# Running the first MLP on the masked tokens alone in a two-MLP block, and its conditioning as rows

## The chip, the cores and the metric

The kernel runs on one core of a Trainium2 chip. The metric is the device time of one execution in microseconds (us); the median of several runs counts. In one profiled execution every instruction was recorded. Its engines are PE (TensorE, the matmuls), DVE (VectorE), ACT (ScalarE), POOL (GpSimd) and SP (SyncE, which only issues transfers); ACT, POOL and SP each have a queue that issues transfers.

## The reference

32 sequences of 128 tokens with 512 features, all float32. A condition vector of each sequence gives six rows of 512: shift, scale and gate for each of two MLPs. The first MLP stands twice (weights `ssm`, `bwd`) and counts only for tokens whose mask is true; the second counts for all.

```python
m = mask[:, :, None]
shift, scale, gate_msa = jnp.split(silu(t) @ ada_w + ada_b, 3, axis=1)
norm = _layernorm(x) * (1.0 + scale[:, None]) + shift[:, None]
norm = jnp.where(m, norm, 0.0)
fwd = _ssm_fallback(norm, ssm_w1, ssm_b1, ssm_w2, ssm_b2)    # gelu(u @ w1 + b1) @ w2 + b2, 512 -> 512 -> 512
bwd = flip(_ssm_fallback(flip(norm), bwd_w1, bwd_b1, bwd_w2, bwd_b2))
x = x + gate_msa[:, None] * jnp.where(m, fwd + bwd, 0.0)
shift_mlp, scale_mlp, gate_mlp = jnp.split(silu(t) @ ffada_w + ffada_b, 3, axis=1)
ff_norm = _layernorm(x) * (1.0 + scale_mlp[:, None]) + shift_mlp[:, None]
h = gelu_tanh(ff_norm @ ff_w1 + ff_b1)                       # 512 -> 1024
return x + gate_mlp[:, None] * (h @ ff_w2 + ff_b2)
```

The mask comes from the setup: a sequence has between 0 and 32 true tokens, its last ones, and over all 32 sequences 499 of the 4096 are true. The mask is an input, so the kernel learns this only while it runs.

## The kernel before

Both MLPs of the first half work token by token, so the kernel joins them into one with a hidden layer of 1024. It works on eight groups of four sequences (512 tokens), and every group goes through both halves in full; the mask only multiplies the result of the first half, in the last step of `mixed` (L256).

`modulation` (L150) computes the conditioning: shift and scale as columns [feature, sequence] (`pm`, L157), the gate as rows (`pg`, L176), which go to DRAM and come back spread over all partitions by `gate_tiles` (L233). `normalise` (L184) does the LayerNorm of four token tiles on DVE, with the square root on ACT. `hidden` (L203) transposes the normalised tiles on PE into `ptr` (L209), lets ACT evict them with scale and shift (L213), and computes the hidden layer `ph` (L225), eight tiles of 128 features by 512 tokens, each a sum of four matmuls; ACT applies the Gelu (L229). `project` (L240) computes `po`, one token tile, as a sum of eight matmuls (L244); DVE adds the bias and multiplies by the gate (L246, L247). In the trace a program's float32 matmul is two PE instructions. Names end in `_a` or `_m` for the first half and `_b` or `_f` for the second.

The program order of the loop is: the first half's projection of group g, its normalising, the hidden layer of the first half of group g + 1, and then the second half of group g. A scheduler of the framework (Tile) turns this into a fixed order for each engine's queue; it also places the waits. SP's queue issues the loads of `ada_w` and of x, ACT's queue the weights, biases and the mask, POOL's queue the gates and the output.

Of the kernel before, what the change touches and what calls it, by code (L numbers as in the profile page):

```python
# [9 lines left out]
F32 = mybir.dt.float32  # L10
U8 = mybir.dt.uint8
AF = mybir.ActivationFunctionType
ALU = mybir.AluOpType

EPS = 1e-6


@with_exitstack
def kernel(
# [35 lines left out]
    B, S, D = x.shape  # L55
    P = 128
# [22 lines left out]

    ident = const.tile([P, P], F32, name="ident")  # L80
    make_identity(nc, ident)
    eps = const.tile([P, 1], F32, name="eps")
    nc.gpsimd.memset(eps, EPS)

# [1 line left out]
    NB = 3 * KC  # L86
    n_bias = 2 * NB + 2 * KC + HC
    t_sb = tp.tile([B, D], F32, tag="t", name="t_sb")
    nc.sync.dma_start(t_sb, cond)
    bias_rows = const.tile([n_bias, P], F32, name="bias_rows")  # L90
    at = 0
    col = {}
    for key, vec in (
        ("ada", ada_b), ("ffada", ffada_b), ("ssm1", ssm_b1), ("bwd1", bwd_b1), ("ff1", ff_b1)
    ):
# [4 lines left out]
    mask_u8 = const.tile([B, S], U8, name="mask_u8")  # L100
    nc.scalar.dma_start(mask_u8, mask)

    def load_ada(w, j, which):
        chunk = adap.tile([P, KC, D], F32, tag="ada", name=f"ada_{which}_{j}")
        nc.sync.dma_start(chunk, w[:, ts(j, D)].rearrange("(k p) f -> p k f", p=P))
        return chunk

    def load_x(g):
        tiles = []
        for i in range(G):  # L110
            t = xp.tile([P, D], F32, tag="x", name=f"x_{g}_{i}")
            nc.sync.dma_start(t, x[g * G + i])
            tiles.append(t)
        return tiles
# [4 lines left out]
    fw2 = const.tile([P, HC, D], F32, name="fw2")  # L119

# [18 lines left out]
    for key in ("ada", "ffada"):  # L139
        c = biasT[:, col[key] + KC : col[key] + 2 * KC]  # L140
        nc.vector.tensor_scalar(c, c, 1.0, None, ALU.add)

# [199 lines left out]
```

## Time and profile before

| | |
|---|---|
| median of 3 runs | 1005.19 us (1004.99 to 1005.72) |
| span of the profiled execution, first to last instruction | 1003.0 us |
| what lies around the span, taken against the median | 2.2 us |
| PE busy | 953.0 us (95%) |
| DVE, ACT, POOL busy | 220.2, 217.2, 30.4 us (22, 22, 3%) |
| PE matmul instructions | 2454 |
| moved by DMA | 49.77 MB |

The busy share tells which engine is full, not what it waits for; the chain that ended last goes back from the last instruction to whatever released each step. "issue" in it is time in which an engine waited for nothing that the profile shows. PEclk is the clock that was granted to TensorE, as a share of 2.4 GHz: 1.0 is the upper of its two levels and 0.5, 1.2 GHz, the lower.

### The profile page before, as it was taken

The numbers are of one execution on the slowest core, as the hardware profiler recorded it, in microseconds if no ns is written. First come the engines' busy times: TensorE is split into PE (matmuls) and PEld (weight loads), VectorE is DVE, ScalarE is ACT, GpSimd is POOL, SyncE is SP. The second block draws the span as 40 slices with busy tenths as digits, with TensorE's granted clock in tenths as the row PEclk, the third lists the DMA queues.
The fourth block names the chain that finished last, engine by engine and source line by source line (L and its number), as shares of the span: only waits on it lengthen the run. The fifth ranks groups of instructions, "written<-read, shape, count | busy, mean of one in ns | idle before, by whom it ended". The sixth has DMA issues, their size and how long they took to land.

```text
span 1003.0 us, 6139 instructions
## 1 busy us (share of the span) xinstructions
PE 953.0 (95%) x2454; PEld 441.0 (44%) x2454; DVE 220.2 (22%) x411; ACT 217.2 (22%) x427; POOL 30.4 (3%) x62
## 2 busy tenths in 40 slices
PE   5699999999999999999999999999999999999796
PEld 5344444444444444444444444444444444444342
DVE  2202500243002510135002430035101430024202
ACT  0220442004410234004410044102340044200310
POOL 1000000000000000000000000000000000000000
PEclk9799999999999999999999999999999999999899
DMA  9921200021002200022000210021000110001000
GB/s 329 356 80 55 74 0 0 32 77 60 0 1 84 70 15 1 21 74 73 1 0 32 84 54 0 11 73 73 1 1 21 63 42 1 0 32 53 0 6 37
DMA packets 16893, 49.77 MB, mean 50 GB/s; under 512 B 1688, under 2 KB 1728, under 8 KB 14816
## 3 DMA queue, kind: packets, MB, share of 16 engines
q0 software_dynamic: 5232, 26.22, 7.4%
q1 hardware_dynamic: 7824, 14.75, 4.4%
q10 hardware_dynamic: 3808, 8.41, 2.3%
q8 instruction: 19, 0.31, 0.1%
q14 instruction: 10, 0.08, 0.0%
HBM read 40.85 MB, written 8.52 MB: 49 GB/s over the span
## 4 chain that ended last, share of the span: by engine, by line
PE 82%; issue 11%; DMA 3%; ACT 2%; POOL 0%; DVE 0%; ACTq 0%; POOLq 0%
PE ph_a L225 22%; PE ph_b L225 19%; PE po_m L244 19%; PE po_f L244 17%; PE ptr_a L209 1%; DMA ada_ffada<-in_L_cond_ffada_w_dram 1%; DMA ada_ada<-in_L_cond_ada_w_dram 1%; ACT xT_b L213 1%; ACT xT_a L213 1%; PE ptr_b L209 1%; PE pm_ada L157 1%; DMA mask_u<-in_mask_BxS_bk_dram 1%; PE pg_ada L176 1%; ACT h_a L229 0%; PE pg_ffada L176 0%
## 5 line engine op out<-in xcount | busy, mean ns | idle before, releaser
L225 PE MATMUL ph_a<-xT_a,w 128*128 128x512 f32 x512 | 226.7, 600 | 0.0
L225 PE MATMUL ph_b<-xT_b,fw 128*128 128x512 f32 x512 | 225.1, 596 | 0.0
L244 PE MATMUL po_m<-w,h_a 128*128 128x512 f32 x512 | 221.1, 592 | 0.0
L244 PE MATMUL po_f<-fw,h_b 128*128 128x512 f32 x512 | 221.0, 592 | 0.0
L244 PEld LDWEIGHTS po_m<-w,h_a 128*128 128x128 f32 x512 | 97.2, 190 | 122.8 <-issue 122.8
L244 PEld LDWEIGHTS po_f<-fw,h_b 128*128 128x128 f32 x512 | 97.3, 190 | 122.5 <-issue 122.5
L225 PEld LDWEIGHTS ph_a<-xT_a,w 128*128 128x128 f32 x512 | 96.3, 192 | 118.7 <-issue 111.4
L225 PEld LDWEIGHTS ph_b<-xT_b,fw 128*128 128x128 f32 x512 | 95.9, 191 | 117.6 <-issue 111.5
L246 DVE TENSOR_TENSOR t_f<-po_f,fb 128x512 f32<-128x512 f32 x32 | 22.1, 692 | 564.8 <-PE po_f L244 564.8
L213 ACT ACTIVATE xT_a<-ptr_a,modT_ada 128x128 f32<-128x128 f32 x128 | 46.4, 465 | 377.0 <-PE ptr_a L209 377.0
L229 ACT ACTIVATE h_b<-ph_b,biasT 128x512 f32<-128x512 f32 x64 | 44.0, 687 | 146.3 <-PE ph_b L225 146.2
L229 ACT ACTIVATE h_a<-ph_a,biasT 128x512 f32<-128x512 f32 x64 | 44.0, 687 | 142.5 <-PE ph_a L225 142.1
L246 DVE TENSOR_TENSOR t_m<-po_m,b 128x512 f32<-128x512 f32 x32 | 22.1, 692 | 128.6 <-PE po_m L244 128.6
L213 ACT ACTIVATE xT_b<-ptr_b,modT_ffada 128x128 f32<-128x128 f32 x128 | 46.3, 477 | 5.7 <-PE ptr_b L209 5.7
L264 POOL DMA_DIRECT2D out_dram<-x x32 | 17.3, 540 | 662.6 <-DVE x L263 661.2
L209 PE MATMUL ptr_b<-ident,xn_b 128*128 128x128 f32 x128 | 19.8, 291 | 15.3 <-ACT xT_b L213 10.9
L209 PEld LDWEIGHTS ptr_b<-ident,xn_b 128*128 128x128 f32 x128 | 15.4, 147 | 26.6 <-ACT xT_b L213 13.0
L209 PE MATMUL ptr_a<-ident,xn_a 128*128 128x128 f32 x128 | 18.8, 281 | 8.5 <-ACT xT_a L213 8.5
L189 DVE BATCH_NORM_STATS2 st_a<-x 128x6 f32<-128x512 f32 x32 | 21.4, 670 | 17.3 <-DMA x<-in_x_dram 17.3
L256 DVE SCALAR_TENSOR_TENSOR x<-t_m,maskT,x 128x512 f32<-128x512 f32 x32 | 24.1, 752 | 1.1
L209 PEld LDWEIGHTS ptr_a<-ident,xn_a 128*128 128x128 f32 x128 | 15.4, 145 | 19.4 <-ACT xT_a L213 11.6
L189 DVE BATCH_NORM_STATS2 st_b<-x 128x6 f32<-128x512 f32 x32 | 22.2, 695 | 1.1
(55 smaller groups left out, 225.1 us busy)
## 6 DMA issues: line engine op xcount, KB each, us to landing
x<-in_x_dram SPq DMA_DIRECT2D x32, 256.0 KB, 5.1
gate_m<-gate_rows_ada POOLq DMA_DIRECT2D x8, 1024.0 KB, 5.2
gate_f<-gate_rows_ffada POOLq DMA_DIRECT2D x8, 1024.0 KB, 5.6
out_dram<-x POOLq DMA_DIRECT2D x32, 256.0 KB, 2.3
fw<-in_L_cond_ff_w_dram ACTq DMA_DIRECT2D x2, 2048.0 KB, 12.3
ada_ada<-in_L_cond_ada_w_dram SPq DMA_DIRECT2D x3, 1024.0 KB, 7.5
ada_ffada<-in_L_cond_ffada_w_dram SPq DMA_DIRECT2D x3, 1024.0 KB, 10.7
w<-in_L_cond_ssm_w_dram ACTq DMA_DIRECT2D x2, 1024.0 KB, 11.7
```

Of the source, the lines that this page charges most:

```text
L157: nc.tensor.matmul(pm[:, ts(j * KC + c, B)], chunk[:, k, ts(c, P)], sT[:, k, :], start=(k == 0), stop=(k == KC - 1),)
L176: nc.tensor.matmul(pg[:B, :], sT[:, k, :], chunk[:, k, :], start=(k == 0), stop=(k == KC - 1))
L189: nc.vector.bn_stats(st, src[i])
L209: nc.tensor.transpose(ptr[:, ts(i, P)], xn[i][:, ts(k, P)], ident)
L213: nc.scalar.activation(t[:, ts(i, P)], ptr[:, ts(i, P)], AF.Identity, bias=modT[:, k, b : b + 1], scale=modT[:, KC + k, b : b + 1],)
L225: nc.tensor.matmul(ph, w[:, k, ts(f, P)], xT[k], start=(k == 0), stop=(k == KC - 1))
L229: nc.scalar.activation(t, ph, func, bias=biasT[:, bcol + f : bcol + f + 1])
L244: nc.tensor.matmul(po, h[f][:, ts(i, P)], w[:, f, :], start=(f == 0), stop=(f == HC - 1))
L246: nc.vector.tensor_tensor(t, po, bias, ALU.add)
L256: nc.vector.scalar_tensor_tensor(r, t, maskT[:, b : b + 1], xt[i], ALU.mult, ALU.add)
L264: nc.gpsimd.dma_start(out[g * G + i], x1[i])
```

## The change

The first half is done once, for 512 slots. At the start the kernel counts the masked tokens of each sequence, computes with small matmuls against triangles of ones at which slot each sequence begins (`first`) and ends (`behind`), and builds `pick`, a matrix of zeros and ones [sequence, slot], four times one above the other so that each strip of 32 partitions has it. `tokens_of` finds the token of each slot, and the reverse, the slot of each token (`slot_i`, a number beyond 512 for a token that is not masked), comes from running sums (`rank`). Four indirect transfers on POOL's queue gather the 512 rows of x.

The conditioning is computed as rows [3 x 32, 512], shift, scale and gate in three strips of 32 columns of PE's array (`modulation`), and spread to the slots by a matmul with `pick` (`of_slots`). The rows of the first half's result go to DRAM (`x1_rows`). Then the eight groups do the second half only: for each group x is loaded, and four indirect transfers put the rows of `x1_rows` over the masked tokens and leave the others as they are (`take_first_half`). The square root becomes a power on POOL. The stores move from POOL's queue to SP's, the loads of the MLP weights from ACT's queue to SP's. At the end stands a loop whose number of trips, (masked tokens - 512 + 127) // 128 and at least 0, is computed on the chip; a trip takes 128 further masked tokens through both halves.

```diff
+    xp = ctx.enter_context(tc.tile_pool(name="xp", bufs=2 * G + 2))
+    xnp = ctx.enter_context(tc.tile_pool(name="xnp", bufs=G + 2))
+    xtp = ctx.enter_context(tc.tile_pool(name="xtp", bufs=2))
...
+    mask_u8 = const.tile([B, S], U8, name="mask_u8")
+    nc.scalar.dma_start(mask_u8, mask)
...
+    def load_ada(w, which):
+        rows = []
+        for k in range(KC):
+            t = adap.tile([P, 3 * D], F32, tag="ada", name=f"ada_{which}_{k}")
+            nc.sync.dma_start(t, w[ts(k, P), :])
+            rows.append(t)
+        return rows
...
+    for j, w in enumerate((ssm_w1, bwd_w1)):
+        nc.sync.dma_start(w1[:, :, ts(j, D)], w.rearrange("(k p) f -> p k f", p=P))
+    for j, w in enumerate((ssm_w2, bwd_w2)):
+        nc.sync.dma_start(w2[:, ts(j, KC), :], w.rearrange("(k p) f -> p k f", p=P))
...
+    count = const.tile([B, 1], F32, name="count")
+    nc.vector.tensor_reduce(count, mask_f, axis=AX.X, op=ALU.add)
+    pb = ps_t.tile([P, 512], F32, tag="tr", name="pb")
+    nc.tensor.transpose(pb[:, :B], mask_f, ident[:B, :B])
+    for j in range(2):
+        nc.tensor.matmul(
+            pb[:, B + j : B + j + 1],
+            upper[:, j].rearrange("p c b -> p (c b)"),
+            count,
+            start=True,
+            stop=True,
+        )
+    nc.tensor.matmul(pb[:, B + 2 : B + 3], ones_b, count, start=True, stop=True)
...
+    pick = const.tile([P, NS], F32, name="pick")
+    nc.vector.scalar_tensor_tensor(pick, slot_row, first, inside, ALU.is_ge, ALU.mult)
...
+    def tokens_of(picked, slots, n, name):
+        pl = ps_t.tile([P, 512], F32, tag="tr", name=f"pl_{name}")
+        for c in range(n):
+            nc.tensor.matmul(pl[:, ts(c, S)], picked[:B, ts(c, P)], rank, start=True, stop=True)
+        view = pl[:, : n * S].rearrange("p (c s) -> p c s", s=S)
+        before = stp.tile([P, n, S - 1], F32, tag=f"before{n}", name=f"before_{name}", bufs=1)
+        nc.vector.tensor_tensor(
+            before,
+            view[:, :, : S - 1],
+            slots.unsqueeze(2).to_broadcast([P, n, S - 1]),
+            ALU.is_le,
+        )
+        token = stp.tile([P, n], F32, tag=f"token{n}", name=f"token_{name}", bufs=1)
+        nc.vector.tensor_reduce(token, before, axis=AX.X, op=ALU.add)
+        nc.vector.tensor_tensor(token, token, view[:, :, S - 1], ALU.add)
+        return token
...
+    def modulation(rows, modb, which):
+        nc.vector.tensor_scalar(modb[B : 2 * B], modb[B : 2 * B], 1.0, None, ALU.add)
         pm = ps_o.tile([P, 512], F32, tag="o", name=f"pm_{which}")
...
         for k in range(KC):
...
+            for j in range(3):
+                nc.tensor.matmul(
+                    pm[ts(j, B), :],
+                    sT[:, k, :],
+                    rows[k][:, ts(j, D)],
+                    start=(k == 0),
+                    stop=(k == KC - 1),
+                )
+        mod = const.tile([3 * B, D], F32, name=f"mod_{which}")
+        nc.vector.tensor_tensor(mod, pm[: 3 * B, :], modb, ALU.add)
+        return mod
+    def of_slots(picked, c, mod, j, pool, tag, name):
+        t = pool.tile([P, 512], F32, tag=tag, name=name)
+        nc.tensor.matmul(
+            t, picked[ts(j, B), ts(c, P)], mod[ts(j, B), :], start=True, stop=True
+        )
+        return t
...
-        rstd = stp.tile([P, G], F32, tag="rstd", name=f"rstd_{name}")
-        nc.scalar.activation(rstd, mv[:, :, 1], AF.Sqrt, bias=eps)
-        nc.vector.reciprocal(rstd, rstd)
+        ve = stp.tile([P, n], F32, tag=f"ve{n}", name=f"ve_{name}")
+        nc.vector.tensor_scalar(ve, mv[:, :, 1], EPS, None, ALU.add)
+        rstd = stp.tile([P, n], F32, tag=f"rstd{n}", name=f"rstd_{name}")
+        nc.gpsimd.tensor_tensor(rstd, ve, half[:, :n], ALU.pow)
...
+    def modulate_slots(xn, picked, c, mod, name):
+        scale = of_slots(picked, c, mod, 1, ps_o, "o", f"sc_{name}")
+        shift = of_slots(picked, c, mod, 0, ps_o, "o", f"sh_{name}")
+        nc.vector.tensor_tensor(xn, xn, scale, ALU.mult)
+        nc.vector.tensor_tensor(xn, xn, shift, ALU.add)
+    def transposed_slots(xn, dst, name):
+        ptr = ps_t.tile([P, 512], F32, tag="tr", name=f"ptr_{name}")
         for k in range(KC):
...
+            nc.tensor.transpose(ptr[:, ts(k, P)], xn[:, ts(k, P)], ident)
+        nc.scalar.copy(dst, ptr.rearrange("p (k s) -> p k s", s=P))
...
+    def hidden(xT, n, w, bcol, func, name):
         h = []
         for f in range(HC):
-            ph = ps_h.tile([P, 512], F32, tag="h", name=f"ph_{name}_{g}_{f}")
+            ph = ps_h.tile([P, 512], F32, tag="h", name=f"ph_{name}_{f}")
             for k in range(KC):
                 nc.tensor.matmul(
-                    ph, w[:, k, ts(f, P)], xT[k], start=(k == 0), stop=(k == KC - 1)
+                    ph[:, :n], w[:, k, ts(f, P)], xT[:, k, :], start=(k == 0), stop=(k == KC - 1)
...
+    def gather(dst, token_col):
+        nc.gpsimd.indirect_dma_start(
+            out=dst,
+            out_offset=None,
+            in_=x_rows,
+            in_offset=bass.IndirectOffsetOnAxis(ap=token_col, axis=0),
+        )
...
+    xc = []
+    for c in range(NC):
+        t = xp.tile([P, D], F32, tag="x", name=f"xc_{c}")
+        gather(t, token_i[:, c : c + 1])
+        xc.append(t)
...
+    mod1 = modulation(ada_k, modb1, "a")
+    ffada_k = load_ada(ffada_w, "f")
+    modb2 = load_mod_bias(ffada_b, "f")
+    nc.sync.dma_start(fw1, ff_w1.rearrange("(k p) f -> p k f", p=P))
+    nc.sync.dma_start(fw2, ff_w2.rearrange("(k p) f -> p k f", p=P))
...
+    xn = normalise(xc, "c")
+    xT_all = xtp.tile([P, KC, NS], F32, tag="xT", name="xT_c")
+    for c in range(NC):
+        modulate_slots(xn[c], pick, c, mod1, f"c{c}")
+        transposed_slots(xn[c], xT_all[:, :, ts(c, P)], f"c{c}")
+    h1 = hidden(xT_all, NS, w1, col["ssm1"], AF.Gelu, "c")
+    x1_rows = dram.tile([NS, D], F32, name="x1_rows")
+    for c in range(NC):
+        gate = of_slots(pick, c, mod1, 2, ps_h, "h", f"gate_c{c}")
+        t = project(c, h1, w2, b2, gate, "c")
+        nc.vector.tensor_tensor(t, t, xc[c], ALU.add)
+        nc.sync.dma_start(x1_rows[ts(c, P), :], t)
+    mod2 = modulation(ffada_k, modb2, "f")
...
+    def take_first_half(g, tiles):
+        for i in range(G):
+            b = g * G + i
+            nc.gpsimd.indirect_dma_start(
+                out=tiles[i],
+                out_offset=None,
+                in_=x1_rows,
+                in_offset=bass.IndirectOffsetOnAxis(ap=slot_i[:, b : b + 1], axis=0),
+                bounds_check=NS - 1,
+                oob_is_err=False,
...
+    xt = load_x(0)
+    take_first_half(0, xt)
+    xT = transposed(0, normalise(xt, "0"))
     for g in range(NG):
-        more = g + 1 < NG
-        if more:
+        if g + 1 < NG:
             xt_next = load_x(g + 1)
-            xn_next = normalise(xt_next, f"a{g + 1}")
-        x1 = mixed(g, xt, h1, gate_tiles(g, rows1, "m"))
-        xn2 = normalise(x1, f"b{g}")
-        if more:
+            take_first_half(g + 1, xt_next)
+        gate = gate_tiles(g)
+        h2 = hidden(xT, G * S, fw1, col["ff1"], AF.Gelu_apprx_tanh, f"f{g}")
+        if g + 1 < NG:
+            xT = transposed(g + 1, normalise(xt_next, f"{g + 1}"))
+        for i in range(G):
+            t = project(i, h2, fw2, fb2, gate[:, i, :], f"f{g}")
+            nc.vector.tensor_tensor(xt[i], xt[i], t, ALU.add)
+            nc.sync.dma_start(out[g * G + i], xt[i])
...
+    more = nc.values_load(
+        more_i[0:1, 0:1],
+        min_val=0,
+        max_val=(T - NS) // P,
+        skip_runtime_bounds_check_because="it is (the masked tokens - NS + 127) / 128, at least 0",
+    )
+    with tc.For_i(0, more, 1):
...
+        xl = xp.tile([P, D], F32, tag="x", name="xl")
+        gather(xl, tok_i)
...
```

## Rows read from the trace of the kernel before

**Rows 1.** The page's head and first busy table: busy us (share of span) xinstructions.

```profile
span 1003.0 us, 6139 instructions
...
PE 953.0 (95%) x2454; PEld 441.0 (44%) x2454; DVE 220.2 (22%) x411; ACT 217.2 (22%) x427; POOL 30.4 (3%) x62
```

**Rows 2.** The page's chain that ended last, shares of the span by engine.

```profile
PE 82%; issue 11%; DMA 3%; ACT 2%; POOL 0%; DVE 0%; ACTq 0%; POOLq 0%
```

**Rows 3.** Groups by line and shape: count | busy us, mean ns | idle before, releaser.

```profile
L225 PE MATMUL ph_a<-xT_a,w 128*128 128x512 f32 x512 | 226.7, 600 | 0.0
L225 PE MATMUL ph_b<-xT_b,fw 128*128 128x512 f32 x512 | 225.1, 596 | 0.0
L244 PE MATMUL po_m<-w,h_a 128*128 128x512 f32 x512 | 221.1, 592 | 0.0
L244 PE MATMUL po_f<-fw,h_b 128*128 128x512 f32 x512 | 221.0, 592 | 0.0
...
L264 POOL DMA_DIRECT2D out_dram<-x x32 | 17.3, 540 | 662.6 <-DVE x L263 661.2 <-issue 1.3
```

**Rows 4.** The chain in order of time, two halves of groups: start us, us, what.

```profile
201.28 27.47 PE po_m L244 x64
...
233.66 25.90 PE ph_a L225 x60
...
264.59 25.96 PE ph_b L225 x60
290.55 27.47 PE po_f L244 x64
318.01 27.47 PE po_m L244 x64
```

**Rows 5.** The chain in order of time, from the start to the first projection.

```profile
17.16 10.36 DMA ada_ada<-in_L_cond_ada_w_dram
...
27.57 5.84 PE pg_ada L176 x8
...
45.25 0.91 PE ptr_a L209 x4
...
84.48 27.66 PE po_m L244 x64
```

**Rows 6.** Windows at the start and the last group: length, engines' busy us (x), PEclk, DMA share, GB/s.

```profile
10.00:25.00 15.00, 13.96 (x65) 13.76 (x65) 4.66 (x13) 0.41 (x1) 0.00 (x0) 1.00 1.04 387
...
912.00:945.00 33.00, 27.19 (x69) 12.51 (x68) 11.13 (x20) 8.06 (x19) 0.00 (x0) 0.90 0.00 0
```

**Rows 7.** Timeline between the halves of the last group: start, us, instruction [idle before].

```profile
929.14 0.69 DVE L246 TENSOR_TENSOR t_m<-po_m,b 128x512 f32<-128x512 f32 x1 [3.71 <-PE po_m L244]
...
932.32 0.30 ACT L192 ACTIVATE rstd_b<-mv_b,eps 128x4 f32<-128x4 f32 x1 [56.13 <-DVE mv_b L190]
...
932.87 1.91 DVE L197 TENSOR_SCALAR xn_b<-x,mv_b,rstd_b 128x512 f32<-128x512 f32 x4
...
933.47 2.06 PE L209 MATMUL ptr_b<-ident,xn_b 128*128 128x128 f32 x8 [4.37 <-DVE xn_b L197]
...
941.10 9.38 PE L225 MATMUL ph_b<-xT_b,fw 128*128 128x512 f32 x21
```

**Rows 8.** Timeline of the last tile.

```profile
987.65 7.03 PE L244 MATMUL po_f<-fw,h_b 128*128 128x512 f32 x16
...
996.17 0.69 DVE L263 TENSOR_TENSOR x<-x,t_f 128x512 f32<-128x512 f32 x1
```

**Rows 9.** DMA issues: queue xcount, KB each, median us from issue to landing.

```profile
x<-in_x_dram SPq DMA_DIRECT2D x32, 256.0 KB, 5.1
...
out_dram<-x POOLq DMA_DIRECT2D x32, 256.0 KB, 2.3
...
mask_u<-in_mask_BxS_bk_dram ACTq DMA_DIRECT2D x1, 4.0 KB, 6.6
```

**Rows 10.** Waits of SP's queue: total us, times, longest; the line is the kernel's end.

```profile
SPq L337 <- PEq L337: 2.2, 2, 1.8
```

**Rows 11.** Waits of PE: total us, times, longest.

```profile
PE ptr_a L209 <- ACT xT_a L213: 8.5, 7, 1.2
```

More of the change, by code (lines that the diff above doesn't have):

```diff
@@ L92 @@
     col = {}
[L93 to L95 removed]
+    for key, vec in (("ssm1", ssm_b1), ("bwd1", bwd_b1), ("ff1", ff_b1)):
         n = vec.shape[0] // P
@@ L99 @@
         at += n
[L100 to L114, printed above, removed]
     w1 = const.tile([P, KC, FF], F32, name="w1")
@@ new lines @@
+    nc.tensor.matmul(pb[:, B + 2 : B + 3], ones_b, count, start=True, stop=True)
+    mcol = const.tile([P, B + 3], F32, name="mcol")
+    nc.vector.tensor_copy(mcol, pb[:, : B + 3])
+    maskT = mcol[:, :B]
+    first, behind, total = (mcol[:, B + j : B + j + 1] for j in range(3))
+    inside = tp.tile([P, NS], F32, tag="t", name="inside")
+    nc.vector.tensor_scalar(inside, slot_row, behind, None, ALU.is_lt)
+    pick = const.tile([P, NS], F32, name="pick")
+    nc.vector.scalar_tensor_tensor(pick, slot_row, first, inside, ALU.is_ge, ALU.mult)
@@ new lines @@
+    pg = ps_t.tile([P, 512], F32, tag="tr", name="pg")
+    nc.tensor.matmul(pg[:B, :S], maskT, lower, start=True, stop=True)
+    rank = const.tile([B, S], F32, name="rank")
+    nc.vector.tensor_scalar(rank, pg[:B, :S], first[:B], None, ALU.add)
+    slot_of = const.tile([B, S], F32, name="slot_of")
+    nc.vector.tensor_scalar(slot_of, rank, -1.0 - FAR, None, ALU.add)
+    nc.vector.tensor_tensor(slot_of, slot_of, mask_f, ALU.mult)
+    nc.vector.tensor_scalar(slot_of, slot_of, FAR, None, ALU.add)
@@ new lines @@
+    mod2 = modulation(ffada_k, modb2, "f")
+    modT = const.tile([P, KC, 3 * B], F32, name="modT")
+    ptr = ps_t.tile([P, 512], F32, tag="tr", name="ptr_mod")
+    for k in range(KC):
+        nc.tensor.transpose(
+            ptr[:, ts(k, 3 * B)], mod2[:, ts(k, P)], ident[: 3 * B, : 3 * B]
+        )
+    nc.vector.tensor_copy(modT.rearrange("p k c -> p (k c)"), ptr[:, : KC * 3 * B])
+    gate_rows = dram.tile([B, D], F32, name="gate_rows")
+    nc.gpsimd.dma_start(gate_rows, mod2[2 * B : 3 * B, :])
@@ new lines, with load_x @@
+    early.close()
+    gp = ctx.enter_context(tc.tile_pool(name="gp", bufs=2))
+    def load_x(g):
+        tiles = []
+        for i in range(G):
+            b = g * G + i
+            t = xp.tile([P, D], F32, tag="x", name=f"x_{g}_{i}")
+            nc.sync.dma_start(t, x[b])
+            tiles.append(t)
+        return tiles
+    def take_first_half(g, tiles):
+        for i in range(G):
+            b = g * G + i
+            nc.gpsimd.indirect_dma_start(
[5 more added lines that the diff above has]
+                oob_is_err=False,
+            )
@@ new lines, in transposed @@
+    def transposed(g, xn):
+        xT = xtp.tile([P, KC, G * S], F32, tag="xT", name=f"xT_{g}")
+        for k in range(KC):
+            ptr = ps_t.tile([P, 512], F32, tag="tr", name=f"ptr_{g}_{k}")
+            for i in range(G):
+                nc.tensor.transpose(ptr[:, ts(i, P)], xn[i][:, ts(k, P)], ident)
+            for i in range(G):
+                b = g * G + i
+                nc.scalar.activation(
+                    xT[:, k, ts(i, P)],
+                    ptr[:, ts(i, P)],
+                    AF.Identity,
+                    bias=modT[:, k, b : b + 1],
+                    scale=modT[:, k, B + b : B + b + 1],
+                )
+        return xT
@@ new lines @@
+        if g + 1 < NG:
+            xT = transposed(g + 1, normalise(xt_next, f"{g + 1}"))
+        for i in range(G):
+            t = project(i, h2, fw2, fb2, gate[:, i, :], f"f{g}")
+            nc.vector.tensor_tensor(xt[i], xt[i], t, ALU.add)
+            nc.sync.dma_start(out[g * G + i], xt[i])
+        if g + 1 < NG:
+            xt = xt_next
+    row_l = const.tile([P, P], F32, name="row_l")
+    nc.vector.tensor_scalar(row_l, slot_row[:, :P], float(NS), None, ALU.add)
+    col_l = const.tile([P, 1], F32, name="col_l")
```

244 lines of the change are left out of this document (133 added, 111 removed).

## The prediction

> **What bounds the kernel now.** I read the page's head and busy table first: PE is busy 95% of the span [rows 1]. The chain of waits gives the same engine: 82% of what ended last is PE, and most of the other 11%, "issue", is PE's spacing between its own matmuls [rows 2]. The groups by line then say on what: four groups of 512 matmuls take 221 to 227 us each, the two layers of the first MLP (ph_a, po_m) and the two of the second (ph_b, po_f), and the two MLPs cost the same [rows 3]. One matmul of the program is two PE instructions, so 512 are 8 groups of sequences x 64.
>
> The chain in order of time gives the rate: 64 po instructions take 27.47 us, 0.429 us each. From one po_m to the next, 318.01 - 201.28 = 116.73 us go by [rows 4]. Of these 4 x 64 x 0.429 = 109.9 us are MLP matmuls and 6.8 us transposes and PE's wait for ACT, which evicts them: 3.4 us for each of the two halves. So a half of a group costs 58.4 us, and only PE's work counts in the steady part: DVE, ACT and POOL are busy at most a quarter of the span [rows 1]. The rest is a start of 112.1 us until the first po_m ends [rows 5], a gap where the last group has no other half beside it [rows 7], and a tail [rows 8].
>
> **The change, part by part.** The mask of the reference's inputs holds 499 true tokens of 4096 (counted from its setup code). They fit in 512 slots, so the computed trip count is (499 - 512 + 127) // 128 = 0, and the loop's body does not run.
>
> *Removed.* Eight first halves become one of 512 slots: 7 x 58.4 = 408.6 us of PE's path go. The Sqrt on ACT goes too, with its table loads; they lay beside PE's work and count for nothing.
>
> *Groups.* Each group is now 64 ph and 64 po, 54.9 us, or 55.1 with the slightly longer ph (27.6). For seven of them the 16 transposes of the next group come between. With today's waits they cost 3.4 us; 1.2 of it PE waits for ACT's evictions [rows 11], so packed they cost 2.2. Today PE has nothing else ready at that place; afterwards the po matmuls of the current group are ready while ACT evicts. I take 2.4, near the packed end: 8 x 55.1 + 7 x 2.4 = 457.6 us (456.2 to 464.6). Under one group lie four loads of x (5.1 us), four gathers, four stores and the normalising of the next group (some 6 us of DVE: four statistics of 0.9, xn 1.9, a power); the hidden layer alone covers 27 us. The stores move from POOL's queue to SP's, where loads queue behind stores that wait for DVE. With ten x buffers the last two loads of group g+1 need the stores of group g-1, and those are out by the middle of that group's projection, so a load is half a group early. On POOL, the gate load and the power for 1/sqrt stand behind gathers that wait for the loads; who waits for them are DVE (xn, then PE's transposes) and the gate multiply, both half a group later. Without this cover, a late gather would be late for the transposes directly.
>
> *Front.* Today the first hidden layer effectively starts 27.6 before its po, near 57 us [rows 5]. Afterwards: the mask is the first transfer on ACT's queue and lands at 3 to 7 us (6.6 us behind six others today [rows 9]). The chain of counting, picking and searching is some 25 DVE and PE steps in turn: four DVE passes over 512 columns at 0.69 [rows 8], 21 short ones at 0.3 (932.32 to 932.87 holds two with their handover [rows 7]), 9 us, and 2 more for PE at the lower clock: 11. The tokens stand at 14 to 19 us, and I take 16. Four gathers of 256 KB: no row has one. Below, it is a plain POOL issue, 0.54 us [rows 3], with the 2.3 us to landing of a 256 KB store; above, each takes 5.1 us like a load of x among other transfers, one behind the other [rows 9]. I take 1.2 us of POOL each, nearer the plain issue because only the row addresses differ, and 4 us to land, since transfers run at 387 GB/s [rows 6] with the weights: all landed at 25. Then the last tile's statistics 0.9, power 0.7, four xn 1.9 [rows 7], eight multiplies and adds from PSUM 5.5, transposes and copy 2: the first hidden layer starts at 36 us (30 to 46).
>
> The conditioning is 24 instructions over 512 columns a time. The row pg_ada, 8 such in 5.84 us, 0.73 each [rows 5], is at a mixed clock; at 0.43 to 0.85 they are 10.3 to 20.5 us in turn. They start as rows of ada_w land, 4 to 12 us, and are done before the first xn is there, at some 27: hidden by the gathers, in the bad case +6 on the front. The first MLP's weights move from ACT's queue to SP's, behind ada_w: 3 + 4 MB at 387 GB/s are 18 us, over before 36.
>
> The Trainium skill (TensorEngine Tiling (Array Packing), Key Properties) says that tiles of the array work independently and in parallel; by that rule the three strips of one k overlap and the 24 cost some 3.4 us at the 0.43 rate. pg_ada is one strip alone, so no row here shows it. By either price the sum is 590, as the gathers end later; by the rule the front's upper end would be 40 instead of 46.
>
> *First half.* 27.6 for ph, 27.5 for po, four gate products of two instructions 3.4, and 3.4 for a PE that restarts at the 1.2 GHz level after idling (clock 0.90 over 33 us is 6.6 us at half rate [rows 6]): 61.9, so until 97.9 us.
>
> *Seam.* The groups need the first half's rows, which now go through DRAM. Today's last group shows the same seam without DRAM: the last po_m is evicted from 929.14 and ph_b streams from 941.10, of which four ph (1.7) are work: 10.4 us lost [rows 7]. The change adds a store (0.4 + 2.3 [rows 9]) and four gathers, 4 x 1.2 + 2.5 = 7.3 (4.5 with plain issues; 20 one behind the other). So 20.4 (14 to 34). The second conditioning, 10.3 us of PE, fits into it, and would cost that much ahead of the projection.
>
> *Tail.* From the last po_f's end, 987.65 + 7.03 = 994.68, to 1003.0 are 8.3 us [rows 8]. The loop of no trips adds reading a number on each engine, synchronising them at its entry and exit and a jump over its body. No row has one. Below it is nothing; the nearest row is the end's own meeting of engines, 2.2 us for two [rows 10]; above I put 15. I take 4.
>
> *Sum.* 36 + 61.9 + 20.4 + 457.6 + 8.3 + 4 = 588.2 us of span. The profiled execution's span is 1003.0 against a median of 1005.2; with these 2.2 us around it: **590 us**, 41% less.
>
> **Rivals.**
> A, the groups wait. If gathers cost POOL 5 us each and start late, or loads stand behind stores on SP, the transposes wait in every group, 5 to 12 us: seven times that is 35 to 84, so 625 to 675 us. For it: four gathers, a power and a gate load in one queue, and SP's mixed order. Against it: the half group of cover. 12%.
> B, front and seam go better than I take them: gathers at the plain issue price, conditioning inside the gaps, a front of 28 and a seam of 12. Then 590 - 8 - 8 - 3 (first half at full clock) - 1 (packed transposes) = 570, down to 558 with no loop cost and a warm start. 15%.
> C, one trip runs because the mask timed holds over 512 tokens. Its chain: tokens and gather some 17, and two halves of some 26 each (64 instructions of 128 columns at a quarter of 0.43 or a little more, 16 of 512, and 10 us of small steps in turn), so about 70: 660 us. Against: 499 counted. 3%.
> D, a dear tail. The loop's entry waits until the last stores have landed, and the jump over the body finds no code ready and waits for a transfer. Two transfers in turn at the dearest small one, 6.6 us [rows 9], are 13 instead of 4: 599 us. For it: nothing lies beside the kernel's end. Against it: no wait of that kind is in the rows. 14%. The Trainium skill (Runtime: NRT & Kernel Launch, Instruction fetch mechanics) speaks for it: code is fetched in sequence, and a taken branch to a page not held waits for a DMA fetch. No row here has a branch, so the trace neither bears it out nor speaks against it.
> E, slower than before: the row gathers. There are 36, four in each group; a group hides about 27 us of them. To lose the whole gain of 415 us, eight groups must each wait 52 us: 79 us for four, some 20 us a gather. The nearest row is 0.54 us of POOL [rows 3] and 2.3 to 5.1 to land [rows 9]. 1%.
>
> **How the numbers follow.** The forecast, 575 to 622, has 55%, and D lies inside its range. The ends of its terms (30 or 46; 14 or 34; 456.2 or 464.6; 0 or 15 for the loop) would not all meet. The low end 566 takes in half of B; the high end 628 stops in A's beginning, so about 17% stays outside. A difference of 0.2% (2 us) is about what a measurement of this kernel can tell from none; all cases but E are far beyond it: faster 98.5%, same 0.5%, slower 1%.
>
> **What would show it.** Right: 64 ph and 64 po instructions for the first MLP and 512 of each for the second; a distance of about 57.5 us from one group's po to the next; one long PE gap between the halves with store, gathers and normalising in it; no instruction of the loop's body. A wait of PE's transposes on xn inside the groups, behind a gather, would show A. Wrong it would be through a gather's price, which stands in the front, the seam and A at once, or through an order of PE's queue that puts the second conditioning ahead of matmuls whose inputs are there.

## The result and the profile after

After: 602.81 us (median of 4 runs, 601.39 to 603.9) against 1005.09, a ratio of 0.5998 [0.5988, 0.6007]: 40% faster. The forecast of 590 is 12.8 us too low; 602.8 lies inside its range of 566 to 628. The loop made no trip.

The page's head and busy table of after:

```profile
span 600.9 us, 3810 instructions
...
PE 547.7 (91%) x1395; PEld 246.7 (41%) x1395; DVE 137.5 (23%) x263; ACT 101.2 (17%) x208; POOL 60.4 (10%) x73
```

The bound is still PE, with 405 us less of busy time than in [rows 1]; its idle time grew from 50 to 53 us and is now in three places. Windows of after, with the columns of [rows 6]: gathering the masked rows, modulating them, the first half, the seam, one group, and the end.

```profile
22.00:36.00 14.00, 8.14 (x30) 1.81 (x24) 4.26 (x11) 0.00 (x0) 4.99 (x5) 0.82 1.03 416
36.00:51.48 15.48, 10.75 (x27) 5.00 (x27) 6.72 (x12) 2.38 (x5) 0.00 (x0) 0.50 0.94 372
51.48:113.27 61.79, 61.79 (x136) 25.71 (x136) 6.21 (x9) 6.74 (x9) 0.00 (x0) 0.97 0.08 26
113.27:140.48 27.21, 11.08 (x49) 5.21 (x49) 14.90 (x34) 4.30 (x12) 14.69 (x15) 0.62 0.32 109
195.76:252.45 56.69, 56.69 (x146) 25.89 (x145) 14.56 (x28) 11.09 (x24) 5.73 (x6) 1.00 0.19 60
590.84:600.90 10.06, 0.00 (x0) 0.00 (x0) 2.08 (x3) 0.00 (x0) 0.00 (x0) 0.67 0.08 29
```

In the first half and in a group PE is busy for every microsecond, nearly all of it at the upper clock level (0.97 and 1.00). Ahead of the first half and in the seam it stands still for long, and runs at the lower level (0.50) when it is needed. The stretches against the prediction's terms, in us:

| term | forecast | measured | from which rows |
|---|---|---|---|
| front, until the first hidden layer | 36 | 51.5 | window 3 begins at 51.48 |
| first half | 61.9 | 61.8 | its length |
| seam | 20.4 | 25.5 | 27.21 less 1.72 for four ph inside |
| groups | 457.6 | 452.1 | 590.84 - 140.48 + 1.72 |
| tail and loop | 12.3 | 10.1 | last window |
| sum (span) | 588.2 | 600.9 | |

**The front.** Timeline of after from the mask to the first hidden layer; a bracket gives the engine's idle time before the instruction and what ended it:

```profile
7.77 0.42 DVE L266 TENSOR_SCALAR modb_a<-modb_a 32x512 f32<-32x512 f32 x1 [4.42 <-DMA modb_a<-in_L_cond_ada_b_dram]
...
10.53 0.42 DVE L266 TENSOR_SCALAR modb_f<-modb_f 32x512 f32<-32x512 f32 x1 [2.34 <-DMA modb_f<-in_L_cond_ffada_b_dram]
10.97 0.20 DVE L195 COPY mcol<-pb 128x35 f32<-128x35 f32 x1
...
18.84 0.69 DVE L367 TENSOR_TENSOR b<-b,b2b 128x512 f32<-128x512 f32 x1 [4.93 <-DMA b2b<-in_L_cond_bwd_b_dram]
...
21.77 0.16 DVE L237 CAST token_i<-token_s 128x4 int32<-128x4 f32 x1
...
26.12 0.95 POOL L352 DMA_INDIRECT xc<-in_x_dram,token_i  x1 [0.30 <-issue]
...
33.40 0.69 DVE L296 BATCH_NORM_STATS2 st_c<-xc 128x6 f32<-128x512 f32 x1 [0.88 <-DMA xc<-in_x_dram,token_i]
...
35.75 1.46 DVE L305 TENSOR_SCALAR xn_c<-xc,mv_c,rstd_c 128x512 f32<-128x512 f32 x3 [1.24 <-POOL rstd_c L301]
...
51.48 5.80 PE L331 MATMUL ph_c<-xT_c,w 128*128 128x512 f32 x9 [0.68 <-ACT xT_c L323]
```

Three instructions that have nothing to do with the tokens stand in DVE's queue among the steps of the token chain: the `+ 1` on the two conditioning biases (L266) and the sum of the first MLP's two output biases (L367). Each waits for a transfer, and the token chain waits behind it: `mcol` starts at 10.97, and the tokens (`token_i`) are there at 21.9. POOL is done with the gathers at 27.1, 5.1 us after the tokens (4.8 forecast), but the last rows are there at 33.4. From the normalised rows to the first hidden layer 15.7 us go by, and DVE waits in it for scale and shift out of PE (its wait rows):

```profile
DVE xn_c L316 <- PE sh_c L284: 3.6, 2, 2.7
DVE xn_c L316 <- PE sc_c L284: 3.2, 1, 3.2
```

**The groups.** Chain in order of time, one period (against 116.73 us for two halves in [rows 4]):

```profile
195.76 27.47 PE ph_f L331 x64
223.23 0.87 PE ptr L430 x8
224.10 1.72 PE po_f L345 x4
225.82 0.44 PE ptr L430 x4
...
252.45 27.47 PE ph_f L331 x64
```

The transposes come in lots between projections, as forecast, and cost 1.75 us (56.69 less two times 27.47). No wait of PE for a gather is in this chain; it is DVE's statistics that wait for the gathers, off the chain.

**The seam.** Timeline of after:

```profile
118.87 1.09 POOL L416 DMA_INDIRECT x<-x_rows,slot_i  x1 [0.31 <-issue]
...
127.63 0.17 DVE L299 TENSOR_SCALAR ve<-mv 128x4 f32<-128x4 f32 x1
...
128.13 1.01 POOL L416 DMA_INDIRECT x<-x_rows,slot_i  x1 [0.30 <-issue]
...
129.75 1.06 POOL L301 TENSOR_TENSOR rstd<-ve,half 128x4 f32<-128x4 f32 x1
...
131.51 2.82 DVE L305 TENSOR_SCALAR xn<-x,mv,rstd 128x512 f32<-128x512 f32 x6
```

POOL's order has the gathers of both the first and the second group (118.87 to 129.14) and a gate load ahead of the first `rstd`, whose input stands at 127.8; and DVE does the second group's statistics ahead of `xn`.

### The profile page after: what moved, and what is told of

The parts are those of the page before. It is cut to its first block, busy times and chain, and to the rows that moved or that the text cites. A ratio compares the mean times of both kernels' runs of the same rounds, so it can differ in the third digit from the quotient of the medians.

```text
span 600.9 us, 3810 instructions
## 1 busy us (share of the span) xinstructions
PE 547.7 (91%) x1395; PEld 246.7 (41%) x1395; DVE 137.5 (23%) x263; ACT 101.2 (17%) x208; POOL 60.4 (10%) x73
## 4 chain that ended last, share of the span: by engine, by line
PE 76%; issue 15%; DMA 4%; DVE 1%; POOL 1%; ACT 0%; SPq 0%; POOLq 0%; DVEq 0%
PE ph_f L331 37%; PE po_f L345 37%; PE ptr L430 3%; DMA xc<-in_x_dram,token_i 1%; DMA b2b<-in_L_cond_bwd_b_dram 1%; DMA ada_a<-in_L_cond_ada_w_dram 1%; DMA modb_f<-in_L_cond_ffada_b_dram 1%; POOL x L416 1%; POOL xc L352 0%; DMA x<-x_rows,slot_i 0%; ACT xT L433 0%; DVE st L296 0%; POOL rstd_c L301 0%; DVE t_f L348 0%; DVE t_f L347 0%
## 5 line engine op out<-in xcount | busy, mean ns | idle before, releaser
L345 PE MATMUL po_f<-fw,h_f 128*128 128x512 f32 x512 | 223.4, 592 | 0.0
L331 PE MATMUL ph_f<-xT,fw 128*128 128x512 f32 x512 | 223.1, 596 | 0.0
L331 PEld LDWEIGHTS ph_f<-xT,fw 128*128 128x128 f32 x512 | 97.6, 191 | 122.3 <-issue 121.6
L345 PEld LDWEIGHTS po_f<-fw,h_f 128*128 128x128 f32 x512 | 95.6, 190 | 112.4 <-issue 112.4
L335 ACT ACTIVATE h_f<-ph_f,biasT 128x512 f32<-128x512 f32 x64 | 44.0, 687 | 337.5 <-PE ph_f L331 337.5
L347 DVE TENSOR_TENSOR t_f<-po_f,fb 128x512 f32<-128x512 f32 x32 | 22.1, 690 | 265.4 <-PE po_f L345 265.4
L416 POOL DMA_INDIRECT x<-x_rows,slot_i x32 | 36.9, 1153 | 285.9 <-DVE t_f L347 220.1
L433 ACT ACTIVATE xT<-ptr,modT 128x128 f32<-128x128 f32 x128 | 45.7, 499 | 54.8 <-PE ptr L430 54.8
L296 DVE BATCH_NORM_STATS2 st<-x 128x6 f32<-128x512 f32 x32 | 22.2, 693 | 86.0 <-DMA x<-x_rows,slot_i 85.9
L331 PE MATMUL ph_c<-xT_c,w 128*128 128x512 f32 x64 | 29.4, 622 | 0.7 <-ACT xT_c L323 0.7
L345 PE MATMUL po_c<-w,h_c 128*128 128x512 f32 x64 | 28.5, 599 | 0.0
L348 DVE TENSOR_TENSOR t_f<-t_f,gate 128x512 f32<-128x512 f32 x32 | 22.2, 695 | 1.1
L462 DVE TENSOR_TENSOR x<-x,t_f 128x512 f32<-128x512 f32 x32 | 22.1, 692 | 1.1
L345 PEld LDWEIGHTS po_c<-w,h_c 128*128 128x128 f32 x64 | 11.8, 190 | 16.4 <-issue 16.4
L347 DVE TENSOR_TENSOR t_c<-po_c,b 128x512 f32<-128x512 f32 x4 | 2.8, 692 | 57.4 <-PE po_c L345 57.4
```

The costliest lines, as they stand in the source:

```text
L296: nc.vector.bn_stats(st, src[i])
L331: nc.tensor.matmul(ph[:, :n], w[:, k, ts(f, P)], xT[:, k, :], start=(k == 0), stop=(k == KC - 1))
L335: nc.scalar.activation(t[:, :n], ph[:, :n], func, bias=biasT[:, bcol + f : bcol + f + 1])
L345: nc.tensor.matmul(po, h[f][:, ts(i, P)], w[:, f, :], start=(f == 0), stop=(f == HC - 1))
L347: nc.vector.tensor_tensor(t, po, bias, ALU.add)
L348: nc.vector.tensor_tensor(t, t, gate, ALU.mult)
```

## The experiments

Ratios are to the kernel before, differences to the 602.8 of after.

**1. DVE's queue.** The waiting instructions go behind the token chain, first each alone, then both:

```diff
-    nc.vector.tensor_copy(token_i, token)
+    tk = nc.vector.tensor_copy(token_i, token)
...
-        nc.vector.tensor_scalar(modb[B : 2 * B], ...)          # e1a, e1c
+        with tc.issue_after(tk.ins):
+            nc.vector.tensor_scalar(modb[B : 2 * B], ...)
...
-    nc.vector.tensor_tensor(b2, b2, b2b, ALU.add)              # e1b, e1c
+    with tc.issue_after(tk.ins):
+        nc.vector.tensor_tensor(b2, b2, b2b, ALU.add)
```

> Edit: the two additions of 1 to the conditioning's biases are queued on DVE behind the step that yields the tokens; nothing else. Queue theory: DVE's queue is in order, and these two wait for their transfers (until 7.77 and 10.53 us) ahead of the copy mcol, whose input PE has ready at 4.9. The whole chain moves up by 6 us: tokens at about 16, first hidden layer at 45.5 instead of 51.5, time 603 - 6 = 597. Transfer theory: the gathers' rows land when the weights' transfers let them, so an earlier issue only waits longer: at most 2 us, 601 to 603.

> Edit: the addition of the two second-layer biases (b2 + b2b) is queued on DVE behind the step that yields the tokens; nothing else. Queue theory: it waits for b2b's transfer from 13.9 to 18.84 us ahead of the search whose input PE has ready at 15.9; without it the tokens stand 3 to 5 us earlier, time 598 to 600. Transfer theory: 601 to 603.

> Edit: both of these moves. Queue theory: 6 + 4 = 10 to 11 us, tokens at about 11 instead of 21.9, first hidden layer at 41, time 592. Transfer theory: the gathers are issued at 11 but their rows land at 30 or later beside 7 MB of weights; time 600 or more.

Measured: 594.95 (0.5913 [0.5903, 0.5923]), 599.45 (0.596 [0.595, 0.597]) and 592.65 (0.5889 [0.5879, 0.5899]): -7.9, -3.4 and -10.2. Timeline with both moved:

```profile
5.18 0.19 DVE L195 COPY mcol<-pb 128x35 f32<-128x35 f32 x1 [1.59 <-PE pb L192]
...
12.49 0.16 DVE L237 CAST token_i<-token_s 128x4 int32<-128x4 f32 x1
...
25.31 1.91 DVE L306 TENSOR_SCALAR xn_c<-xc,mv_c,rstd_c 128x512 f32<-128x512 f32 x4 [1.24 <-POOL rstd_c L302]
```

The tokens stand 9.3 us earlier and the whole kernel ends 9.5 us earlier by the spans (591.4). So the queue's order was the cause of these 9.3 us, and the gathers, started among the first loads, took no longer for it (6.0 us to land, 6.7 in after; medians of the four).

**2. PSUM tiles of the modulation.** Shift takes its tiles from another pool, so that scale and shift no longer share three:

```diff
-        shift = of_slots(picked, c, mod, 0, ps_o, "o", f"sh_{name}")
+        shift = of_slots(picked, c, mod, 0, ps_h, "h", f"sh_{name}")
```

> Edit: the shift product of each slot tile takes a buffer of the hidden layer's PSUM pool instead of the output pool's three; nothing else. Buffer theory: DVE waits 6.8 us for scale and shift products, which wait for buffers that DVE has not freed; with six buffers most are there before xn, and the first hidden layer comes 4 us earlier: 599. Clock theory: PE runs this stretch at the 1.2 GHz level (0.50 granted from 31 to 55 us) and its 27 instructions there take 10.8 of 15.5 us whatever the buffers: 0 to 2 us, 601 to 603.

598.94 (0.5948 [0.5935, 0.596]), -3.9. From `xn_c` at 36.73 to the first hidden layer at 47.92 are 11.2 us instead of 15.7: 4.5 of the 6.3 above the forecast 9.4 were PE and DVE waiting for each other's tiles.

**3. Loads beside the gathers.**

```diff
     xn = normalise(xc, "c")
+    with tc.issue_after(rstd_ins[0].ins):                   # the first rstd
+        ffada_k = load_ada(ffada_w, "f", nc.gpsimd)
+        nc.gpsimd.dma_start(fw1, ...)
+        nc.gpsimd.dma_start(fw2, ...)
```

> The loads of the second half's conditioning weights and MLP weights are issued by POOL behind the first rstd instead of by SP at the start; nothing else changes. Theory (the gathers of the masked rows land in 6.7 us because these loads keep the DMA engines at a share of 1.0 just then): the gathers land in about 3 us, as the gathers of the later groups do (2.8), the first hidden layer starts about 4 us earlier, and the time is about 599. Rival (the gathers' landing is their own, or what the stretch gains is spent by the conditioning product on PE, which ends no earlier): within 1 us of 602.8. If the late loads are late for the seam, it is slower.

602.21 (0.5987 [0.5975, 0.5999]): no change. The gathers land in 6.0 us, and the DMA engines stay full (share 1.05 from 22 to 28 us), now with the second weight matrix and rows of x.

Then the same on SP's queue, with the second weight matrix too, ahead of the loads of x:

```diff
+    with tc.issue_after(rstd_ins[0].ins):
+        nc.sync.dma_start(w2[:, ts(j, KC), :], ...)         # j = 0, 1
+        ffada_k = load_ada(ffada_w, "f")
+        nc.sync.dma_start(fw1, ...)
+        nc.sync.dma_start(fw2, ...)
```

> All loads of SP that the first hidden layer does not need (the first half's second weight matrix, the second half's conditioning and MLP weights, and the first groups' rows of x) are issued behind the first rstd. In the run with only the second half's weights late, the DMA engines were still full while the masked rows were gathered (landing 6.0 us). Contention theory: now the gathers run nearly alone and land in about 3 us, the first hidden layer starts about 3 us earlier, 599 to 600. Rival (the landing is the gathers' own when the rows come from x): 6 us as before, and 602 to 603. Slower, if the late weights are then late for the second product of the first half or for the seam.

604.38 (0.601 [0.6, 0.6019]), +1.6. This run does not answer its question. Its trace shows SP issuing the second weight matrix at 11.53 and the other weights from 24.13 on: an order given between SP's queue and POOL's made no wait, and nothing was late. The last run (8) repeats it within POOL's own queue.

**4. The order in the seam.**

```diff
-            take_first_half(g + 1, xt_next)
-        gate = gate_tiles(g)
+            with tc.issue_after(rstd_ins[1 + g].ins):    # rstd of group g
+                take_first_half(g + 1, xt_next)
+        with tc.issue_after(rstd_ins[1 + g].ins):
+            gate = gate_tiles(g)
```

> In every group the next group's gathers and the group's own gates are put behind the group's rstd in POOL's order. Theory (at the seam the first group's rstd and normalisation stand in queue behind the second group's gathers and statistics): the stretch from the last product of the first half to the second half's hidden layers shrinks by about 4 us of its 25.5, groups unchanged, about 599. Rival (only the 2 us that rstd waits in POOL's queue come back, or the x rows themselves come last): 0 to 2 us, 601 to 603. If the later gathers are then late in the groups: slower by up to some us in each.

600.91 (0.5976 [0.5966, 0.5986]), -1.9. Its timeline:

```profile
127.77 0.17 DVE L301 TENSOR_SCALAR ve<-mv 128x4 f32<-128x4 f32 x1
128.02 1.04 POOL L303 TENSOR_TENSOR rstd<-ve,half 128x4 f32<-128x4 f32 x1 [2.92 <-DVE ve L301]
...
138.32 8.24 PE L333 MATMUL ph_f<-xT,fw 128*128 128x512 f32 x18
```

`rstd` follows `ve` at once. The last product of the first half ended here at 114.46, so the seam is 138.32 - 114.46 - 1.72 = 22.1 instead of 25.5: the mechanism gave 3.4 of the 4 expected. The time gained only 1.9, since the first half took 62.8 (51.64 to 114.46) instead of 61.8. Windows of 54.9 to 57.4, in after and in this kernel, show where:

```profile
54.90:57.40 2.50, 2.50 (x7) 1.14 (x6) 0.00 (x0) 0.51 (x1) 0.00 (x0) 1.00 0.00 0
```

```profile
54.90:57.40 2.50, 2.50 (x4) 0.94 (x3) 0.00 (x0) 0.00 (x0) 0.00 (x0) 0.56 0.00 0
```

The clock rose some 2.2 us later, which at half pace is the 1 us. The total alone would have spoken for the rival; the stretch decides.

**5. The strips.** All three parts in one strip, 24 products as before:

```diff
-        pm = ps_o.tile([P, 512], F32, tag="o", name=f"pm_{which}")
+        pm = [ps_o.tile([P, 512], F32, tag="o", name=f"pm_{which}{j}") for j in range(3)]
...
-                    pm[ts(j, B), :],
+                    pm[j][:B, :],
```

> The three parts of each conditioning product (scale, shift, gate) are all put out in the first column strip, into three PSUM tiles, instead of in three strips of one tile; the same 24 products of the same shapes. Theory (instructions in different strips run side by side): the first conditioning product takes about three times as long at the lower clock, some 18 to 20 us instead of 6.6, the second 10 to 11 instead of 3.6; the front grows by 6 to 8 us, as part of the first lies beside the gathers, and the seam by up to 6: 609 to 616. Rival (they run in turn either way and the speed of the strips is no part of the front): 602 to 604.

608.4 (0.6048 [0.6033, 0.6062]), +5.6, just below the theory's 609 to 616. Timelines: the second conditioning in after, then in this kernel.

```profile
113.27 3.63 PE L270 MATMUL pm_f<-ada_f,sT 128*32 128x512 f32 x24
```

```profile
21.34 12.94 PE L270 MATMUL pm_a<-ada_a,sT 128*32 128x512 f32 x24
...
117.82 10.49 PE L270 MATMUL pm_f<-ada_f,sT 128*32 128x512 f32 x24
```

Same 24 instructions: 3.63 us in three strips, 10.49 in one. The first conditioning takes 12.94 instead of 6.59, less than the expected 18 to 20, because PE changed to the faster pace during it. The edit does two things more: the three parts take all three tiles of their PSUM pool, and three additions on DVE (2.10 us) stand in the place of one (0.69). So the 5.6 us are the price of this edit as a whole; the length of the second conditioning alone shows what the strips do.

**6. Cover of the gathers.** The gathers of six groups are issued twice:

```diff
             take_first_half(g + 1, xt_next)
+            if g + 1 >= 2:
+                take_first_half(g + 1, xt_next)
```

> The gathers of the groups from the third on are issued twice, into the same tiles: 24 more gathers, with the same output. Theory (a group's gathers are done some 29 us before its transposes need the rows, so that they have cover): within 1 us of 602.8. Rival (the groups wait for POOL's gathers): about 4 x 1.3 us more in each of six groups, 620 to 634.

605.66 (0.6025 [0.6014, 0.6036]), +2.9: more than the theory's 1, far from the rival's 17. Where is it? One group by windows:

```profile
197.01:253.70 56.69, 56.69 (x146) 25.89 (x145) 13.60 (x25) 11.07 (x24) 10.13 (x10) 1.00 0.19 58
```

POOL works 10.1 us instead of 5.7, and the group takes 56.69 as before. By the profile 1.3 us were already lost ahead of the second group (a later rise of the clock in the first half, as in run 4), and 1.9 come at the end, behind the last product (12.0 instead of 10.1). The groups have the cover. The longer end stands in SP's last wait for PE (6.7 us instead of 4.8, see run 7); why that wait grew stays open.

**7. The loop and its trip.** First without it:

```diff
-    with tc.For_i(0, more, 1):
-        ...
```

> The loop at the end is left out, with what it prepares; with 499 masked tokens in 512 slots it makes no trip, so that the output is the same here, but not for more than 512 masked tokens. Theory from the terms of the tail (10.06 us from the last product to the end, against 8.3 in the kernel before): about 1.8 us less, 601. Rival (the code behind the loop has to be brought in, 4 us and more): 597 to 599. Rival (all of it lies beside the last stores): no change.

595.61 (0.5924 [0.5914, 0.5933]), -7.2, more than any theory said; the rival with the fetched code (597 to 599) came nearest. By the profile (span 594.5), 1.7 of it is the front: without the loop's preparations the scheduler put all of the token chain but its last step ahead of the waiting bias sum. The rest is the end: the last product ends at 589.15, so the tail is 5.35 instead of 10.06. The loop costs 4.7 us here. The DMA queues for code in the last 13 us of after:

```profile
q8 instruction: 1, 0.02, 0.6%
q14 instruction: 1, 0.01, 0.1%
```

and all DMA queues in the last 13 us of the kernel without the loop:

```profile
q1 hardware_dynamic: 288, 0.52, 10.6%
```

With the loop code is fetched twice there (q8, q14); without it not at all. SP's wait for PE at the end of after follows; before it was 2.2 us in all [rows 10], and without the loop it is 0.7:

```profile
SPq L561 <- PEq L561: 4.8, 2, 4.3
```

Then with one trip:

```diff
-    NS = 512
+    NS = 384
```

> 384 slots instead of 512: with 499 masked tokens the loop now makes one trip for the other 115. What a trip costs was put at 70 us, worked out from before's rows at one tile of 128 tokens through both halves. The first half has a quarter fewer slots: its products, one in four of 61.8 us, save about 15, and the front one tile of modulation, some 2 to 3. Expected: 602.8 + 70 - 17 = 656, with 640 to 675. Rival (a trip, with its serial chain of gathers, normalisation and transposes at the lower clock, costs twice that): 710 and more.

637.51 (0.6342 [0.6332, 0.6351]), just below the range of 640 to 675. Its timeline around the trip:

```profile
565.68 0.69 DVE L347 TENSOR_TENSOR t_f<-po_f,fb 128x512 f32<-128x512 f32 x1 [4.73 <-PE po_f L345]
...
568.49 0.29 DVE L480 TENSOR_SCALAR in_l<-row_l,mcol 128x128 f32<-128x128 f32 x1 [0.67 <-DVE x L462]
...
571.32 1.01 POOL L352 DMA_INDIRECT xl<-in_x_dram,tok_i  x1 [114.91 <-DVE to_i L491]
...
574.64 0.69 DVE L296 BATCH_NORM_STATS2 st_l<-xl 128x6 f32<-128x512 f32 x1 [3.35 <-DMA xl<-in_x_dram,tok_i]
...
600.44 0.69 DVE L296 BATCH_NORM_STATS2 st_l<-xl 128x6 f32<-128x512 f32 x1
...
625.60 1.06 POOL L508 DMA_INDIRECT out_dram<-xl,to_i  x1 [23.43 <-DVE xl L507]
```

From the last product (565.66) to the end (634.1) 68.4 us go by, 58.4 more than in after: the price of a trip. Its two halves are the forecast 26 each (574.64 to 600.44, and on to 625.3); tokens and gather are 6.2, not 17. The smaller first half saves 24 instead of 17: the front ends at 42.0 and the first half takes 47.1.

The trip also holds what run 3 asked for: a gather of masked rows from x (L352, as in the front) with the DMA engines nearly free (share 0.27 from 571.3 to 574.7 us). It landed in 2.8 us. In the front the gathers by this line took 5.8 to 7.0 us in every run (medians), at a share of 1.0.

**8. All together.** Edits 1, 2 and 4, and the loads that the first hidden layer does not need in POOL's queue behind the first `rstd`:

```diff
+    with tc.issue_after(rstd_ins[0].ins):
+        for j, w in enumerate((ssm_w2, bwd_w2)):
+            nc.gpsimd.dma_start(w2[:, ts(j, KC), :], w.rearrange("(k p) f -> p k f", p=P))
+        ffada_k = load_ada(ffada_w, "f", nc.gpsimd)
+        nc.gpsimd.dma_start(fw1, ...)
+        nc.gpsimd.dma_start(fw2, ...)
...
+    with tc.issue_after(rstd_ins[0].ins):
+        xt = load_x(0)                                      # on POOL's queue
```

> All edits that should help, together: both DVE instructions that wait for transfers behind the token chain, the shift's products in the other PSUM tiles, POOL's order in the groups, and, new and this time in POOL's own queue behind the first rstd, every load that the first hidden layer does not need (second weight matrix, second conditioning weights, second MLP weights, the first group's rows of x), so that the masked rows are gathered with little beside them. If the gains of the earlier runs add up (10.2, 3.9 and 1.9 us by their medians), 587 without the late loads. Contention theory: the gathers then land in 3 us instead of 6 to 7, and it is 583 to 585. Rival (the landing is the gathers' own): 6 us as before, 586 to 588. Rival (the gains overlap, as the half-rate stretch and the transfers are shared): 589 to 593.

584.75 (0.5821 [0.581, 0.5833]): 18 us less than after, the fastest version. A window (columns as above) and the timeline:

```profile
18.00:22.00 4.00, 2.31 (x12) 0.83 (x14) 2.12 (x5) 0.00 (x0) 0.08 (x1) 1.00 1.04 413
```

```profile
17.12 0.96 POOL L353 DMA_INDIRECT xc<-in_x_dram,token_i  x1 [0.30 <-issue]
18.04 1.06 PE L269 MATMUL pm_a<-ada_a,sT 128*32 128x512 f32 x6 [0.54 <-DMA ada_a<-in_L_cond_ada_w_dram]
...
23.04 0.69 DVE L297 BATCH_NORM_STATS2 st_c<-xc 128x6 f32<-128x512 f32 x1 [0.43 <-DMA xc<-in_x_dram,token_i]
...
25.39 2.06 DVE L306 TENSOR_SCALAR xn_c<-xc,mv_c,rstd_c 128x512 f32<-128x512 f32 x4 [1.24 <-POOL rstd_c L302]
...
36.72 9.51 PE L332 MATMUL ph_c<-xT_c,w 128*128 128x512 f32 x17 [0.67 <-ACT xT_c L324]
```

The late loads now really are late, yet the rows still take 5.9 us (17.12 to 23.04) and `xn_c` starts at 25.39, as in run 1 (25.31): until 22 us the engines are full with what the first hidden layer itself needs (the last rows of `ada_w` come at 18.04, then its weights) and two tiles of x of the second group, which SP still loads from 12.07 on. So this run, too, did not give the gathers free engines, and that its time lies in the contention theory's range of 583 to 585 does not speak for that theory. The gains of 1, 2 and 4 add up: 10.2 + 3.9 + 1.9 = 16.0, measured 18.1 by the medians. By the spans it is 16.4: 14.8 less in the front, 3.3 less in the seam, and an end that is 1.4 longer, again in SP's last wait (5.9 us).

## Why the prediction came out as it did

- **The total: inside the range, in part by luck.** The front (+15.5) and the seam (+5.1) came out dearer, the groups (-5.5) and the end (-2.2) cheaper; the 12.8 us are what is left of some 28 us of errors.
- **Removed work, first half: the mechanism right, the close agreement luck.** 61.8 against 61.9, but two terms are off by 1.6 us each way. `ph` runs from 51.48 to 80.81, 1.9 us longer than the 27.47 of a group: so much the restart at the lower clock cost (0.50 until 54.9), not 3.4. The four rounds of gate products and `po`, 80.81 to 113.27, take 32.46, 5.0 more than 27.47: so much the gate products cost, not 3.4.

```profile
80.81 1.12 PE L284 MATMUL gate_c<-mod_a,pick 32*128 32x512 f32 x2
```

- **Front: the step that failed.** 36 became 51.5. The mask landed early (2.9 us), and the token chain's work was sized well: 9.7 us from mask to tokens in run 1, 11 forecast. But the prediction counted the chain's own instructions and not what else stands in DVE's queue. The waits for transfers ahead of them cost 9.3 of the 15.5 (run 1, where the chain is also faster than forecast). The gathers' POOL price was right (1.0 + 0.3 gap, 1.2 forecast), their landing too low: 6.7 instead of 4. The power on POOL, put at 0.7 without a row, took 1.05. And the modulation was counted as DVE's 5.5 us, not as DVE and PE passing three PSUM tiles to and fro with PE at the lower clock: 15.7 instead of 9.4 from `xn_c` on (4.5 of the difference by run 2). Against the forecast's own steps: tokens 5.9 later, the rows there another 2.5, from there to the first hidden layer 7.1 more. With runs 1 and 2 put in (run 8), the front is 36.7.
- **What the landing hangs on: most likely the full DMA engines.** It is 5.8 to 7.0 us in the front of every run, where the engines are full, 2.8 for the groups' gathers from `x1_rows` (share 0.19 over a group), and 2.8 for the one gather of masked rows from x with the engines nearly free (run 7). So the landing is not the gathers' own when the rows come from x. That is one gather of 128 rows, not four in a row; what the front would gain was not measured, as no edit freed the engines there.
- **Seam: +5.1.** 3.4 of it is the second group's gathers in POOL's order ahead of the first `rstd` (run 4), in the place where the prediction had looked only at the price of four gathers. The other 1.7 is not traced. (The loss read from [rows 7] is 941.10 - 929.14 - 1.7 = 10.3, not 10.4.)
- **Groups: -5.5.** The forecast 55.1 + 2.4 was measured as 54.9 + 1.75: the transposes pack better than the packed end of the estimate (2.2), and `ph` takes 27.47, not 27.6.
- **Tail and loop: two errors that cancel in part.** The loop was put at 4 and costs 4.7. The other 8.3 were taken from [rows 8] and are 5.35 without a loop. The difference lies behind the last store's issue: 3.2 us to the end without the loop, through SP's queue (591.34 to 594.5), 5.8 before, through POOL's (997.16 to 1003.0). That the queue of the stores makes it was not tried alone.
- **Strips.** The Trainium skill (TensorEngine Tiling (Array Packing), Key Properties) says that tiles of the array work in parallel. Run 5 agrees: 3.63 us in three strips, where the prediction's estimate by that rule was 3.4, and 10.49 in one, where its price in turn was 10.3. That this would be hidden by the gathers either way was wrong: run 5's edit cost 5.6 us, 3.5 of it in the front (first hidden layer at 55.0, in part by DVE's two further additions) and the rest behind it.
- **Rivals.** A is false: doubled gathers left the group at 56.69. B did not come: even run 8 has a front of 36.7 and a seam of 22.2, not 28 and 12. C did not arise; a trip costs 58 us, not 70. D had the place right and the price too high: 4.7 instead of 13. The Trainium skill (Runtime: NRT & Kernel Launch, Instruction fetch mechanics) says that a taken branch to a page not held waits for a fetch. Two code fetches in the tail with the loop and none without it agree (before has one, q14, in its last 13 us), but how much of the 4.7 they make was not separated. E is false by 1.0 us of POOL for a gather against the 20 it needed.

## What to carry to other kernels

When a short chain of small steps becomes the start of everything, list all instructions of each queue ahead of its links, above all those that wait for a transfer: here three additions of 0.4, 0.4 and 0.7 us of work held up 600 us of kernel by 10. Compare stretches between the same two events, not totals, when an edit is worth less than what the clock's rise moves. And price a loop of zero trips as something: here 4.7 us, in a place where nothing lies beside it.

## What was unexpected of the hardware

PE's first conditioning ran at half pace while the granted clock of that stretch shows 1.00. From the views of one tile in after (minimum/median/maximum in ns):

```profile
L270 PE MATMUL pm_a<-ada_a,sT x24: 603/1061/1062, 21.6 to 27.6; 128*32 128x512 f32 x24
...
L270 PE MATMUL pm_f<-ada_f,sT x24: 592/592/617, 113.3 to 116.3; 128*32 128x512 f32 x24
```

PE was little used before it (2.83 of the 9.5 us from 12.0 to 21.5). So 1.00 in the row of a stretch need not mean that PE already runs at the upper level's pace: in run 5 the weight loads of `pm_a` are 0.85 us apart until 26.4 us and 0.43 from then on, with 1.00 granted throughout. No run here shows why.
